# The late slot tiles of a routed layer: more DMA transposes, probabilities folded into the rows, ReLU and sum as one operation of VectorE

## The chip, the cores and the metric

The kernel runs on one core of one Trainium2 chip. A core has five engines: TensorE (PE for its products, PEld for its weight loads), VectorE (DVE), ScalarE (ACT), GpSimd (POOL) and SyncE (SP). All DMAs, from whichever engine's queue, are carried by 16 DMA engines. Time is the device time of one execution in microseconds (us), and lower is better.

## The reference

Two layers run over x of 2 x 2048 rows of 512. Each is a cross attention to a context of 128 rows and a feed forward part, with residual sums. Only the last part matters here, the feed forward part of the second layer, in which each row is sent to one of eight experts:

```python
xn = (x - mean) / sqrt(var + 1e-5)
probs = softmax(xn @ Wg + bg)
idx = argmax(probs)
p = probs[idx]
e = idx % 8
h = relu(xn @ We[e] + be[e])
x = x + h * p
```

The probability p is positive, so p * relu(z) equals relu(p * z). Everything is fp32 in this part.

## The kernel before, in words

There are 32 tiles of 128 rows (NT), called x tiles, and they stay in SBUF (xw, 516 columns each: 512 of data, then the mean, the reciprocal deviation, the probability p and a zero). The first layer and the second layer's attention run over these tiles until about 1440 us. A finished tile is written to a buffer in DRAM (x_dram), with its four extra columns.

The rows are then put in order by expert. A *slot tile* is 128 rows that all belong to one expert; there are 39 of them, numbered j = 0 to 38 here and called slots. The first NJA = 15 are formed when 22 of the 32 x tiles are done (routing(True)) and hold full slots only; the other 24 (NJB) are formed at the end (routing(False)), and there an expert's last slot can be partly empty, and the last slots wholly. For each slot the routing gives the expert's number, the rows to fetch (row), and the place in the output of each (tok). The change sets in at LATE = NJA + 3 = slot 18.

The work on a slot is spread over several turns of expert(j), which are unrolled. The order on TensorE, VectorE, ScalarE and GpSimd is the program's own order (a manual schedule); only semaphores hold an instruction back. SP's queue has the DMA transposes.

- gathered(j + 4), L1157 to L1162: GpSimd issues an indirect DMA that fetches slot j + 4's rows, with their mean, deviation and probability, into one of six buffers (xw[0] to xw[5]).
- turned_x2(j + 1), L1178 to L1185: slot j + 1's centred rows come into transposed form (128 features on the partitions, in four blocks). There are two ways. In the first, TensorE transposes four 128x128 blocks (L116) and ScalarE evicts them from PSUM (L1185), adding RAISE = 4.0 to the first feature of each block by a bias column. In the second, by_dma(j), the rows have gone through a DMA transpose (which works on 16-bit data: split, L825 to L829, lets VectorE part the fp32 words into halves and SP issue the transpose), and ScalarE joins the halves (joined, L831). Before the change every odd slot from 5 on goes this way.
- the product, L1193 to L1195: four blocks of 128 features times the expert's weights, each fp32 product in two passes, so eight matmuls a slot into one PSUM bank of 512 columns (pz). The expert's bias is not added in a separate step: RAISE makes the first feature of each block larger by 4, and the weights have had rows added that carry the bias to match.
- centered_x(j + 3), L1164 to L1172: VectorE centres and scales slot j + 3's rows (L104 in center). For a slot that goes by DMA it then adds RAISE to four columns (L1171), and calls split.
- the end of slot j, L1197 to L1203: ScalarE computes relu(p * z) from PSUM (L1198), VectorE adds x (L1199), GpSimd issues an indirect DMA that scatters the rows to the output (L1200). Empty places have a row number beyond the output and are left out by the DMA.

On VectorE, then, slot j's sum stands behind slot j + 3's centring, RAISE and split. On GpSimd's queue gathers and scatters take turns: gather j + 4, scatter j, gather j + 5, scatter j + 1. The scatters all write the tensor out, and the gathers all read x_dram. The PSUM banks for transposes and products come from one pool of four buffers (psm, tag m).

Of the kernel before, what the change touches and what calls it, by code (L numbers as in the profile page):

```python
# [16 lines left out]
U16 = mybir.dt.uint16  # L17
I8 = mybir.dt.int8
AF = mybir.ActivationFunctionType
ALU = mybir.AluOpType  # L20
# [4 lines left out]
P = 128  # L25
B, S, T, D = 2, 2048, 128, 512
ND = D // P
# [16 lines left out]
NJA = NTA - (NE - 1)  # L44
# [4 lines left out]
RAISE = 4.0  # L49
# [14 lines left out]
def two_layers(ctx: ExitStack, tc: tile.TileContext, a, out):  # L64
    nc = tc.nc
# [16 lines left out]
    raised = const.tile([P, 1], F32, name="raised")  # L82
# [3 lines left out]
    xw = [xres.tile([P, DX], F32, name=f"x{n}") for n in range(NT)]  # L86
# [16 lines left out]
    def center(dst, x, mean, scale):  # L103
        nc.vector.tensor_scalar(dst, x, mean, scale, ALU.subtract, ALU.mult)  # L104
# [7 lines left out]
    def transposed(psum, src, n=ND):  # L112

        pt = psum.tile([P, n, P], F32, name="pt", tag="m")
        for c in range(n):
            nc.tensor.transpose(pt[:, c, :], src[:, c * P : (c + 1) * P], ident)  # L116
        return pt
# [707 lines left out]
    def split(x, planes):  # L825
        nc.vector.tensor_copy(
            planes.rearrange("p (h f) -> p h f", h=2), x.bitcast(U16).rearrange("p (f h) -> p h f", h=2)
        )
        nc.sync.dma_start(out=x.bitcast(U16).rearrange("p (b q) -> p b q", q=P), in_=planes, transpose=True)  # L829

    def joined(dst, x):  # L831
        nc.scalar.copy(  # L832
            dst.bitcast(U16).rearrange("p c (q h) -> p h c q", h=2),
            x.bitcast(U16).rearrange("p (h c q) -> p h c q", h=2, c=ND),
        )
# [181 lines left out]
    def part(n, shape, dtype=F32, at=0):  # L1017

        size = math.prod(shape)
        v = xw[n][:, at : at + (size * mybir.dt.size(dtype) + 3) // 4]  # L1020
        if dtype is not F32:
            v = v.bitcast(dtype)[:, :size]
        if len(shape) == 1:
            return v
        names = "abc"[: len(shape)]
        return v.rearrange(f"p ({' '.join(names)}) -> p {' '.join(names)}", **dict(zip(names, shape)))
# [128 lines left out]
    ring = {}  # L1155

    def gathered(j):  # L1157
        if j < NJ:
            nc.gpsimd.indirect_dma_start(
                out=xw[j % 6], out_offset=None, in_=x_dram[: (NTA if j < NJA else NT) * P, :],  # L1160
                in_offset=bass.IndirectOffsetOnAxis(ap=tile_of[j][2], axis=0),
            )  # L1162

    def centered_x(j):  # L1164
        if j < NJ:
            x = xw[j % 6]
            xn = part(6 + j % 3, [D])
            center(xn, x[:, :D], x[:, D : D + 1], x[:, D + 1 : D + 2])
            if by_dma(j):
                first = xn.rearrange("p (c q) -> p c q", c=ND)[:, :, 0:1]  # L1170
                nc.vector.tensor_scalar(first, first, RAISE, None, ALU.add)  # L1171
                split(xn, part(24 + j // 2 % 2, [2 * D], U16))  # L1172

    def by_dma(j):

        return j > 4 and j % 2 == 1

    def turned_x2(j):  # L1178
        if j < NJ and by_dma(j):
            ring[j] = part(9 + j % 3, [ND, P])  # L1180
            joined(ring[j], part(6 + j % 3, [D]))
        elif j < NJ:
            pt = transposed(psm, part(6 + j % 3, [D]))
            ring[j] = part(9 + j % 3, [ND, P])
            nc.scalar.activation(ring[j], pt, AF.Identity, bias=raised)  # L1185

    def expert(j):

        te, tok, _ = tile_of[j]
        gathered(j + 4)  # L1190
        turned_x2(j + 1)
        e = nc.tensor.value_load(te, min_val=0, max_val=NE - 1)
        pz = psm.tile([P, D], F32, name="pz", tag="m")  # L1193
        for c in range(ND):
            nc.tensor.matmul(pz, ring[j][:, c, :], we[:, bass.ds(e, 1), c, :], start=(c == 0), stop=(c == ND - 1))  # L1195
        centered_x(j + 3)
        x, acc = xw[j % 6], part(12 + j % 3, [D])  # L1197
        nc.scalar.activation(acc, pz, AF.Relu, scale=x[:, D + 2 : D + 3])  # L1198
        nc.vector.tensor_tensor(acc, acc, x[:, :D], ALU.add)  # L1199
        nc.gpsimd.indirect_dma_start(  # L1200
            out=out_rows, out_offset=bass.IndirectOffsetOnAxis(ap=tok, axis=0),
            in_=acc, in_offset=None, bounds_check=NT * P - 1, oob_is_err=False,
        )  # L1203
# [32 lines left out]
    for n in range(NT):  # L1236
# [55 lines left out]
        if not ahead:  # L1292

            expert(n - NT + NB1)
# [18 lines left out]
        if n == NT - NB1 - 1:  # L1313
            for j in range(3):
                centered_x(j)
            turned_x2(0)
# [4 lines left out]
    picked(NT - 2)  # L1321
    gated(NT - 2)()
    expert(2)
    turned2(NT - 1)
    expert(3)
    logits(NT - 1)
    picked(NT - 1)
# [48 lines left out]
```

## Time and profile before

| what | value |
|---|---|
| time, median of 3 runs | 1597.74 us (1596.93 to 1598.61) |
| time of the profiled execution | 1599.43 us |
| its span, first to last instruction | 1597.4 us |
| granted TensorE clock, mean | 0.995 |
| PE, DVE, ACT, POOL busy over the span | 97%, 75%, 45%, 37% |
| first and last product of a slot (L1195) | 1408.7 and 1586.8 us |
| last scatter issued | 1589.12 us |
| slot 18's first product | 1507.7 us |

The span runs from the first to the last instruction; the time of an execution also has what lies around it (2.0 us here). A line of the timeline gives the start, the duration, the engine, the line of the program, the operation, the names out<-in, their shapes where there are any, and a count; in brackets stands how long the engine was idle before it and what ended that. Names such as x stand for any of the xw tiles: gathered rows, centred rows, transposed rows and sums all lie in them, so the line number tells them apart. A line such as L104 or L826 stands in a helper that several parts call.

### The profile page before, as it was taken

The page shows a single profiled execution, that of the slowest core. Times are in us where ns is not written, and L with a number is a line of the kernel's source. Part 1 is how long each engine was busy: PE and PEld are TensorE (multiplying, and loading weights), DVE is VectorE, ACT ScalarE, POOL GpSimd, SP SyncE. Part 2 cuts the span into 40 slices and gives each one's busy share as a digit, 9 for nine tenths or more (in the row PEclk, how much of TensorE's full clock was granted, in tenths as well). Part 3 has the DMA queues.
Part 4 walks back from the last instruction along what each step waited for, and adds up shares of the span by engine and source line. Part 5 has one row for each costly group of instructions (what it writes and reads, how often), then busy time and mean ns, then how long its engine had stood idle before and what let it go on. Part 6 is the DMA issues. An engine that isn't in the chain of part 4 may idle for free. (4 is left out here: it accounts for less than half of the span.)

```text
span 1597.4 us, 26167 instructions
## 1 busy us (share of the span) xinstructions
PE 1551.3 (97%) x9542; PEld 909.1 (57%) x9542; DVE 1192.5 (75%) x2333; ACT 720.4 (45%) x1537; POOL 586.8 (37%) x580
## 2 busy tenths in 40 slices
PE   7999999999999999999999999999999999999997
PEld 5655555555555555544444466666666666654443
DVE  3467777777777886589986678888888888877442
ACT  1222222222222222243335566777777776763442
POOL 2232222222222222110005654555565444544553
PEclk9999999999999999999999999999999999999999
DMA  9511212111111220367768734221311111114553
GB/s 321 188 37 41 47 40 47 40 47 40 51 46 41 59 60 1 117 169 205 179 173 278 271 132 143 48 47 34 55 45 36 41 28 41 41 47 131 162 162 89
DMA packets 180571, 150.90 MB, mean 94 GB/s; under 512 B 97089, under 2 KB 144665, under 8 KB 180444
## 3 DMA queue, kind: packets, MB, share of 16 engines
q1 hardware_dynamic: 170188, 127.25, 28.5%
q0 software_dynamic: 6240, 18.70, 3.8%
q10 hardware_dynamic: 4016, 3.29, 0.9%
q8 instruction: 76, 1.25, 0.3%
q14 instruction: 51, 0.42, 0.1%
HBM read 89.97 MB, written 41.79 MB: 82 GB/s over the span
## 5 line engine op out<-in xcount | busy, mean ns | idle before, releaser
L419 ACT ACTIVATE pr<-sc 128x1024 f32<-128x1024 f32 x64 | 65.6, 1024 | 421.6 <-PE sc L414 421.4
L393 PE MATMUL pq<-xnT,wq 128*128 128x256 f32 x1024 | 254.4, 391 | 0.0
L451 PE MATMUL pw<-wo,att 128*128 128x512 f32 x512 | 230.8, 593 | 0.0
L393 PEld LDWEIGHTS pq<-xnT,wq 128*128 128x128 f32 x1024 | 184.4, 189 | 67.1 <-issue 44.0
L914 ACT ACTIVATE s<-s,mx 128x128 f32<-128x128 f32 x512 | 175.3, 388 | 28.1 <-DVE mx L905 28.1
L923 POOL TENSOR_TENSOR s<-s,rs 128x1024 f32<-128x1024 f32 x64 | 120.9, 1903 | 149.6 <-DVE rs L922 149.1
L403 POOL TENSOR_TENSOR q<-rt,rt 128x256 f32<-128x256 f32 x64 | 46.7, 730 | 339.7 <-DVE rt L402 335.2
L451 PEld LDWEIGHTS pw<-wo,att 128*128 128x128 f32 x512 | 96.9, 190 | 96.4 <-issue 89.9
L441 DVE RECIPROCAL rd<-sc 128x256 f32<-128x256 f32 x64 | 112.4, 1757 | 46.5 <-PE sc L435 46.5
L1195 PE MATMUL pz<-we,x 128*128 x312 | 139.3, 598 | 1.8 <-ACT x L832 1.6
L872 PE MATMUL pq<-xT,wq 128*128 128x256 f32 x512 | 122.6, 382 | 0.0
L978 PE MATMUL pl<-wgate,xnT 128*128 128x512 f32 x256 | 116.7, 599 | 0.0
L955 PE MATMUL pw<-wo,oT 128*128 128x512 f32 x256 | 115.2, 592 | 0.7 <-ACT oT L946 0.7
L872 PEld LDWEIGHTS pq<-xT,wq 128*128 128x128 f32 x512 | 96.0, 190 | 33.1 <-issue 20.3
L398 DVE TENSOR_TENSOR rt<-pq,rope_cos 128x256 f32<-128x256 f32 x64 | 27.0, 422 | 104.2 <-PE pq L393 104.2
L749 ACT ACTIVATE gate<-pg,gsc 128x512 f32<-128x512 f32 x88 | 60.5, 687 | 93.9 <-PE pg L744 84.0
L1195 PEld LDWEIGHTS pz<-we,x 128*128 128x128 f32 x312 | 58.2, 192 | 68.4 <-issue 65.2
L92 DVE BATCH_NORM_STATS2 st<-x 128x6 f32<-128x512 f32 x130 | 89.4, 688 | 6.0 <-DMA x<-in_ctx 3.8
L744 PE MATMUL pu<-xqT,wuT 128*128 128x512 bf16 x352 | 90.3, 379 | 2.6 <-DVE h L752 2.4
L744 PE MATMUL pg<-xqT,wgT 128*128 128x512 bf16 x352 | 90.3, 379 | 0.0
L900 DVE SCALAR_TENSOR_TENSOR s<-sc,keep 128x1024 f32<-128x1024 f32 x64 | 78.1, 1220 | 14.3 <-PE sc L892 9.1
L955 PEld LDWEIGHTS pw<-wo,oT 128*128 128x128 f32 x256 | 48.6, 190 | 55.3 <-issue 53.6
(226 smaller groups left out, 2811.8 us busy)
## 6 DMA issues: line engine op xcount, KB each, us to landing
h_dram<-h SPq DMA_DIRECT2D x88, 256.0 KB
hq<-h_dram SPq DMA_DIRECT2D x31, 704.0 KB
x_dram<-x SPq DMA_DIRECT2D x32, 258.0 KB
x<-in_x SPq DMA_DIRECT2D x32, 256.0 KB
we<-in_L_ffn_We SPq DMA_DIRECT2D x8, 1024.0 KB
xnT<-in_x_turned SPq DMA_DIRECT2D x14, 512.0 KB
along<-stat_dram SPq DMA_DIRECT2D x14, 256.0 KB
w_in<-in_L_ffn_w_gate SPq DMA_DIRECT2D x11, 256.0 KB
```

Source lines behind the costliest of these rows:

```text
L92: nc.vector.bn_stats(out=st, in_=x)
L393: nc.tensor.matmul(pq, wqs[c // 2][:, c % 2, par, g * P : (g + 1) * P], xnTs[k][:, c, :], start=(c == 0), stop=(c == ND - 1))
L441: nc.vector.reciprocal(rd, sc[:, 0, B0:])
L451: nc.tensor.matmul(pw, atts[u][:, f, t * P : (t + 1) * P], wo[:, 2 * g + f, :], start=(g == 0 and f == 0), stop=(g == NG - 1 and f == 1),)
L744: nc.tensor.matmul(dst, w[:, c, i * P : (i + 1) * P], xqTs[blk][:, c, :], start=(c == 0), stop=(c == ND - 1),)
L872: nc.tensor.matmul(pq, wq1[:, c, f * P : (f + 1) * P], xTs[blk][:, c, :], start=(c == 0), stop=(c == ND - 1))
L900: nc.vector.scalar_tensor_tensor(s, sc[:, 2 * half : 2 * half + 2].rearrange("p r c k -> p (r c) k"), -MASKED, keeps[n].unsqueeze(1).to_br ...
L914: nc.scalar.activation(s[:, h, :], s[:, h, :], AF.Exp, bias=mx[:, h : h + 1], **accum)
L923: nc.gpsimd.tensor_tensor(s, s, rs.unsqueeze(2).to_broadcast([P, 8, T]), ALU.mult)
L955: nc.tensor.matmul(pw, os_[n][:, c, :], wo1[:, c, :], start=(c == 0), stop=(c == ND - 1))
L978: nc.tensor.matmul(pl, xn2T[n][:, c, :], wgate[:, c, :], start=(c == 0), stop=(c == ND - 1))
L1195: nc.tensor.matmul(pz, ring[j][:, c, :], we[:, bass.ds(e, 1), c, :], start=(c == 0), stop=(c == ND - 1))
```

## The change

It touches slots 18 to 38 alone.

- Which slots go by DMA: there j % 3 > 0 (19, 20, 22, 23, ... 37, 38), where it was the odd ones. The halves' buffers become three (24 + j % 3) in place of two.
- The probability is multiplied into the rows: VectorE forms scale times probability in the spare column (rp), and centring uses it, so that the product is already p * z. What RAISE adds must then be p * RAISE, and it is added to the rows by VectorE in every slot (scalar_tensor_tensor on four columns), not only in those that go by DMA; ScalarE's eviction of a TensorE transpose (L1185) becomes a plain copy.
- ReLU and sum: in place of ScalarE's activation (L1198) and VectorE's sum (L1199) there is one scalar_tensor_tensor of VectorE, max(pz, 0) + x, which reads PSUM.

```diff
+    LATE = NJA + 3
+
     def centered_x(j):
+
         if j < NJ:
-            x = xw[j % 6]
-            xn = part(6 + j % 3, [D])
-            center(xn, x[:, :D], x[:, D : D + 1], x[:, D + 1 : D + 2])
+            x, xn = xw[j % 6], part(6 + j % 3, [D])
+            r, p = x[:, D + 1 : D + 2], x[:, D + 2 : D + 3]
+            first = xn.rearrange("p (c q) -> p c q", c=ND)[:, :, 0]
+            if j >= LATE:
+                rp = x[:, D + 3 : D + 4]
+                nc.vector.tensor_tensor(rp, r, p, ALU.mult)
+                center(xn, x[:, :D], x[:, D : D + 1], rp)
+                nc.vector.scalar_tensor_tensor(first, p.to_broadcast([P, ND]), RAISE, first, ALU.mult, ALU.add)
+            else:
+                center(xn, x[:, :D], x[:, D : D + 1], r)
+                if by_dma(j):
+                    nc.vector.tensor_scalar(first, first, RAISE, None, ALU.add)
             if by_dma(j):
-                first = xn.rearrange("p (c q) -> p c q", c=ND)[:, :, 0:1]
-                nc.vector.tensor_scalar(first, first, RAISE, None, ALU.add)
-                split(xn, part(24 + j // 2 % 2, [2 * D], U16))
+                split(xn, part(24 + j // 2 % 2 if j < LATE else 24 + j % 3, [2 * D], U16))
 
     def by_dma(j):
 
-        return j > 4 and j % 2 == 1
+        return j % 3 > 0 if j >= LATE else j > 4 and j % 2 == 1
 
     def turned_x2(j):
...
             ring[j] = part(9 + j % 3, [ND, P])
-            nc.scalar.activation(ring[j], pt, AF.Identity, bias=raised)
+            if j >= LATE:
+                nc.scalar.copy(ring[j], pt)
+            else:
+                nc.scalar.activation(ring[j], pt, AF.Identity, bias=raised)
 
     def expert(j):
...
         x, acc = xw[j % 6], part(12 + j % 3, [D])
-        nc.scalar.activation(acc, pz, AF.Relu, scale=x[:, D + 2 : D + 3])
-        nc.vector.tensor_tensor(acc, acc, x[:, :D], ALU.add)
+        if j >= LATE:
+            nc.vector.scalar_tensor_tensor(acc, pz, 0.0, x[:, :D], ALU.max, ALU.add)
+        else:
+            nc.scalar.activation(acc, pz, AF.Relu, scale=x[:, D + 2 : D + 3])
+            nc.vector.tensor_tensor(acc, acc, x[:, :D], ALU.add)
```

## The prediction

> **Views, and what bounds the kernel.** I read the page first, its engine shares.
>
> ```profile
> PE 1551.3 (97%) x9542; PEld 909.1 (57%) x9542; DVE 1192.5 (75%) x2333; ACT 720.4 (45%) x1537; POOL 586.8 (37%) x580
> ```
>
> TensorE looks like the bound of the whole, but the change acts only from slot 18 on, so I read that stretch alone. Slots are found by counting: there are 39 scatters of L1200, the one at 1589.12 is slot 38. Slot 18's gathered rows are centred at 1500.47. Next comes the table by stretches, cut at the PE transposes, so that each row holds two slots (stretch, its length, busy time of PE, PEld, DVE, ACT, POOL, clock, DMA share, GB/s).
>
> ```profile
> 1504.30:1511.60 7.30, 7.30 (x22) 3.42 (x21) 3.05 (x6) 3.28 (x5) 3.78 (x4) 1.00 0.61 177
> ...
> 1563.60:1571.90 8.30, 7.50 (x22) 3.39 (x20) 3.16 (x6) 3.11 (x5) 4.48 (x5) 1.00 0.60 161
> 1571.90:1580.20 8.30, 7.57 (x20) 3.46 (x20) 3.16 (x6) 3.12 (x5) 3.44 (x4) 1.00 0.51 124
> ```
>
> At the start of the stretch TensorE has no gap and two slots take 7.30; at its end two slots take 8.30 with the same work. Something else has become late by then. The waits from 1475 to the end (total us, times, longest) say what:
>
> ```profile
> DVE x L104 <- DMA x<-x_dram,x: 52.6, 26, 2.9
> POOL out_x L1200 <- DMA out_x<-x,x: 18.4, 11, 2.2
> ACT x L832 <- DMA x<-x: 15.7, 10, 2.6
> DVE x L1199 <- ACT x L1198: 9.9, 7, 3.2
> PEld pz L1195 <- ACT x L832: 2.6, 4, 1.1
> ```
>
> VectorE waits for gathers, and scatters wait for the scatter before them: each scatter writes the same output tensor, so each is held until its predecessor has landed. Gather and scatter take turns on POOL's queue, so a late scatter delays the next gather. POOL's timeline shows the pace:
>
> ```profile
> 1510.87 1.05 POOL L1200 DMA_INDIRECT out_x<-x,x  x1 [2.12 <-DMA out_x<-x,x]
> 1512.23 1.35 POOL L1159 DMA_INDIRECT x<-x_dram,x  x1 [0.30 <-ACT x L1198]
> 1514.49 1.02 POOL L1200 DMA_INDIRECT out_x<-x,x  x1 [0.91 <-DMA out_x<-x,x]
> ...
> 1518.43 1.02 POOL L1200 DMA_INDIRECT out_x<-x,x  x1 [1.52 <-DMA out_x<-x,x]
> ...
> 1522.20 1.02 POOL L1200 DMA_INDIRECT out_x<-x,x  x1 [1.46 <-DVE x L1199]
> ```
>
> These are the scatters of slots 17, 18, 19 and 20, at intervals of 3.62, 3.94 and 3.77. Over all scatters from slot 16 (1506.44) to 35 (1580.09) the interval after an even slot is 4.15 (ten, sum 41.49), after an odd slot 3.57 (nine, sum 32.16). TensorE needs 7.30 / 2 = 3.65 a slot. So **the ring of scatters is the bound from about slot 16**, TensorE trails it, and by the last four slots stands still for it. Even slots are slower because just before scatter j VectorE splits slot j+3, which is odd and goes through the DMA transpose, whose transfer then flies beside the scatter. One round, with slot 27 brought in and slot 24 written:
>
> ```profile
> 1529.54 1.02 POOL L1200 DMA_INDIRECT out_x<-x,x  x1 [1.08 <-DVE x L1199]
> 1530.87 0.98 POOL L1159 DMA_INDIRECT x<-x_dram,x  x1 [0.30 <-ACT x L1198]
> ...
> 1534.64 0.60 DVE L104 TENSOR_SCALAR x<-x 128x512 f32<-128x512 f32 x1 [2.47 <-DMA x<-x_dram,x]
> ...
> 1535.27 0.17 DVE L1171 TENSOR_SCALAR x<-x 128x4 f32<-128x4 f32 x1
> 1535.47 0.79 DVE L826 COPY x<-x 128x1024 uint16<-128x1024 uint16 x1
> 1536.18 0.67 DVE L1199 TENSOR_TENSOR x<-x,x 128x512 f32<-128x512 f32 x1
> ...
> 1537.13 1.02 POOL L1200 DMA_INDIRECT out_x<-x,x  x1 [1.38 <-DVE x L1199]
> ...
> 1539.89 1.35 ACT L832 COPY x<-x 128x1024 uint16<-128x1024 uint16 x1 [1.65 <-DMA x<-x]
> ```
>
> The second loop is seen here: scatter 22 to gather 27 1.33, to its centring 3.77, centring to split 0.83, to the sum 0.71, the sum 0.67, to scatter 24 0.28: 7.59 for two slots, nearly the 4.15 + 3.57 = 7.72 of the ring. Both loops bind in turn.
>
> **The change, part by part** (slots 18 to 38).
>
> Fewer transposes on TensorE. Of these 21 slots 11 were turned by TensorE, now 7 (18, 21, ... 36). Four transposes lie between 1503.87 and the next product at 1504.31, 0.44; four slots save 1.76. I count it as nothing: what hides it is TensorE's own lateness behind the ring. Had TensorE the lead, it would be worth 1.76.
>
> More slots by DMA: 14 in place of 10, so four more splits (0.69 each, VectorE), four more transposes in SP's queue (from issue at 1536.40 to the joining at 1539.89, 3.49), four more joinings (1.34, ACT) in place of four evictions (0.68, ACT). Nothing else stands in SP's queue after 1455; ACT waits 45.1 us for products in this stretch, so its work is covered. What is on the path is the slower kind of scatter interval. Those with a DMA slot three ahead were 10 of the 19 intervals of slots 16 to 34; now they are slots 16, 17, 19, 20, 22, 23, 25, 26, 28, 29, 31, 32 and 34, 13 of 19. 3 x (4.15 - 3.57) = **+1.74**. This assumes that two DMA slots in a row disturb no more than single ones; from below, if the difference came from the order of slots alone, 0.
>
> The split is where a page speaks against the change. The row: the gather at 1512.23 took 1.35 beside a split (0.69 from 1512.05), others 0.98. The Trainium skill (SBUF — State Buffer, Who interferes with whom) says that a VectorE copy in its two-port mode holds the port pair that GpSimd shares, and GpSimd is blocked for the whole instruction. By the rule four more splits could hold four queue entries for up to 0.69, 2.8 in all; by the row 4 x 0.37 = 1.5. Neither is added here.
>
> The product of scale and probability, on one column. An operation on 128x1 takes 0.15 (L986), and the one that reads its result as a scalar starts 0.19 after it (L1002 at 1441.60, L1003 at 1441.79). It stands between the gather's landing and the centring, so it lengthens the second loop by 0.19 in each slot. The raise of the first columns as a scalar_tensor_tensor is priced by L1145's 0.18, against 0.17 at L1171 for DMA slots; for TensorE's slots it is new, 0.20 with its start, where the loop has over 0.8 to spare (no split).
>
> ReLU and sum as one operation of VectorE. No row has just this; L956 (PSUM and SBUF, 128x512) takes 0.69, L821 (scalar_tensor_tensor, 128x512) 0.75. I take 0.70, nearest to L956, against 0.69 for L1199. ScalarE's L1198 goes (21 x 0.68). In the body it isn't worth anything: slot 24's ReLU started at 1533.63, right behind its product, and its sum at 1536.18, held by centring and split. The waits on L1198 (9.9) that it would remove fell before slot 18. The sum now waits for TensorE itself; behind it stand the next slot's product, centring and split, and it is ready long before. The PSUM buffer is freed by the sum, some 2.75 later (slot 32: ReLU ends 1564.09, sum 1566.84); with four buffers, and four taken in three slots, product 33 (1563.63) would need slot 30's sum, done at 1558.89. 4.7 to spare, so nothing.
>
> So the second loop grows by 0.19 + 0.01 a DMA slot. From below 0, where the ring binds; from above 0.20 for each two slots over 18 slots, 1.8. The ring of two slow intervals is 8.3, the loop 7.6 to 7.8, so most is hidden: **+0.5**.
>
> The end. Slot 38 is now a DMA slot. Its centring started at 1577.79, when the gather had landed; + 0.19 + 0.58 + 0.20 + 0.69 + 0.14 gives an issue at 1579.6; 3.5 (as slot 27) to 4.3 (slot 37, issued 1574.53, joined from 1578.87) and the joining 1.34 give a product at 1584.4 to 1585.3, before 1583.79: +0.6 to +1.5. Then ReLU and sum, 1587.43 to 1588.84, 1.41, become 0.73: -0.68. **Between -0.1 and +0.8, I take +0.3**.
>
> Sum: 1.74 + 0.5 + 0.3 = **+2.5**. The profiled execution took 1599.43, its span 1597.4 and 2.0 around it; the span would be 1599.9. The median of the runs, 1597.74, is 1.7 below the profiled time; 1597.74 + 2.5 = **1600.2**.
>
> **Rivals.** *TensorE is the bound after all.* For it: no gap at TensorE until 1563. Against: scatters at 3.86 a slot against its 3.65. Then 1.76 and the 0.68 at the end come through: 1595.3; if the 2 x 1.0 of the last two pairs went too, 1593.3. It decides if scatter intervals fall below 3.6.
>
> *The DMA transposes get in each other's way* (slower). Two DMA slots follow each other at 3.9, and a transpose takes 3.5 to 4.3 from issue to joining. From scatter j-5 to scatter j by way of the transpose: 1.33 + 3.77 + 0.19 + 0.63 + 0.20 + 0.93 + 3.49 + 1.35 + 0.05 + product and its end 3.7 + 0.70 + 0.28 = 16.6 for five slots, 3.3 each: spare 2.9. It decides from 6.4 a transpose on. At 7.0 (two in line) 20.1 / 5 = 4.02 in place of 3.86, 20 slots x 0.16 = 3.2 more: 1603.4. For it: the 4.3 of slot 37. Against: the DMA share is 0.6, not 1.
>
> *The disturbance is no matter of transposes*, and the added VectorE work is covered: 1597.74 to 1598.2. For it: the two kinds of interval are read from one order of slots, in which even and odd never change places. Against: ten of ten even intervals are longer than the odd ones beside them.
>
> **How the numbers follow.** Forecast 0.50 (its own range 1598.7 to 1602.3), TensorE 0.18, transposes in line 0.22, no effect 0.10. What a measurement of this kernel can tell from no change is about 0.2%, 3.2 us: 1594.5 to 1600.9. Of the forecast about 0.32 lie within that and 0.18 above; of the TensorE case 0.12 below and 0.06 within. Faster 0.12, same 0.32 + 0.06 + 0.10 = 0.48, slower 0.18 + 0.22 = 0.40. The range takes the transposes' case to 1604 and half the TensorE case, to 1594.5.
>
> **What would show it.** Right: scatters about 3.95 apart, longer after slots with a DMA slot three ahead; three slots on TensorE 11.5 to 12 where its work is 10.7; more waiting of TensorE for L832's successor; product to first sum unwaited. Wrong: intervals below 3.7 and a TensorE without gaps (faster), transposes of 6 and more from issue to joining (slower), or a sum much above 0.75.

## The result, and the profile after

The changed kernel takes 1601.49 us in the median of 21 runs, the kernel before 1598.26 in 21 runs beside them: a ratio of 1.0018, 95% interval 1.0012 to 1.0025, so it is slower by 2.9 us (1.9 to 4.0). The forecast was +2.5. One execution in a later run, of the changed kernel with views, took 3219.12 and is left out of its ratio. The profiled execution's span is 1599.6, before 1597.4. From slot 18's first product (1507.08, before 1507.74) to the end of the span it takes 92.5, before 89.7: +2.9, so the time is lost in the slots that the change touches.

The engine shares of the page hardly move:

```profile
PE 1549.6 (97%) x9526; PEld 904.7 (57%) x9526; DVE 1199.8 (75%) x2369; ACT 709.3 (44%) x1516; POOL 585.6 (37%) x580
```

TensorE has 1.7 us less work (four transposed slots, forecast 1.76), ScalarE 11.1 less, VectorE 7.3 more, and yet the time rises. The table by stretches, now of three slots each because that is the new rhythm (stretch, its length, busy time of PE, PEld, DVE, ACT, POOL, clock, DMA share, GB/s):

```profile
1507.10:1517.80 10.70, 10.70 (x29) 4.92 (x28) 5.92 (x14) 3.95 (x4) 5.96 (x6) 1.00 0.55 150
1517.80:1530.80 13.00, 11.24 (x29) 4.90 (x28) 5.87 (x14) 3.11 (x3) 5.84 (x7) 1.00 0.63 166
1530.80:1542.90 12.10, 11.34 (x30) 4.91 (x29) 5.84 (x14) 3.11 (x3) 5.56 (x6) 1.00 0.61 153
...
1566.30:1578.10 11.80, 11.23 (x30) 4.92 (x29) 5.96 (x14) 3.27 (x3) 6.05 (x6) 1.00 0.67 174
```

The first three slots take 10.70 without a gap, which is the pace that the saved transposes allow; every later three take 11.6 to 13.0. Before, TensorE had hardly a gap until 1563; now gaps stand in every stretch from 1517.80 on. The busy times of 11.0 to 11.3 beside a need of 10.7 also hold short waits between products. The waits from 1475 to the end:

```profile
ACT x L832 <- DMA x<-x: 41.7, 11, 6.0
DVE x L1175 <- DMA x<-x_dram,x: 39.8, 21, 4.0
POOL out_x L1217 <- DVE x L1213: 22.4, 12, 2.9
...
PEld pz L1209 <- ACT x L832: 12.0, 11, 1.8
POOL out_x L1217 <- DMA out_x<-x,x: 10.7, 7, 2.2
```

The scatters' waits have to be read beside a line of the kernel before that the prediction doesn't show. It stands in the same view as the others, above the ring's 18.4:

```profile
POOL out_x L1200 <- DVE x L1199: 22.1, 16, 2.3
```

Two shifts matter. The wait of TensorE's weight loads for joined rows rose from 2.6 to 12.0. And the scatters' waits moved further to the sum: for the scatter before, eleven waits (18.4) have become seven (10.7), while from slot 18 on twelve scatters (22.4) wait for VectorE's new sum (L1213). In the same views from 1505 on the kernel before has ten waits for the scatter before (16.7) and eleven for the sum (13.9), the changed one seven (10.7) and fourteen (25.5, L1213 and the two of L1216). The second loop of the prediction, gather to sum, bound about as often as the ring before; now it binds twice as often. One round, with slot 26 brought in and slot 23 written:

```profile
1526.83 1.02 POOL L1217 DMA_INDIRECT out_x<-x,x  x1 [2.66 <-DVE x L1175]
1528.15 1.06 POOL L1159 DMA_INDIRECT x<-x_dram,x  x1 [0.30 <-issue]
...
1528.43 18.61 SPq L829 DMA_TRANSPOSE x<-x  x4
...
1530.37 1.02 POOL L1217 DMA_INDIRECT out_x<-x,x  x1 [1.16 <-DMA out_x<-x,x]
...
1533.00 0.16 DVE L1175 TENSOR_TENSOR x<-x 128x1 f32<-128x1 f32 x1 [4.05 <-DMA x<-x_dram,x]
1533.26 0.55 DVE L104 TENSOR_SCALAR x<-x 128x512 f32<-128x512 f32 x1
1533.46 1.33 ACT L832 COPY x<-x 128x1024 uint16<-128x1024 uint16 x1 [5.75 <-DMA x<-x]
...
1534.65 0.68 DVE L1213 SCALAR_TENSOR_TENSOR x<-pz,x 128x512 f32<-128x512 f32 x1
...
1535.61 1.02 POOL L1217 DMA_INDIRECT out_x<-x,x  x1 [2.94 <-DVE x L1213]
```

The row of SPq stands for four issues merged into one; the first is at 1528.43. The round took 8.78 for two slots, where the round shown of before took 7.59. The gather of 1528.15 needed 4.85 to VectorE's first instruction (before 3.77), and the transpose issued at 1528.43 was joined only at 1533.46, after 5.03 (before 3.49). Both were in flight at once, and the scatter of 1530.37 came between. From scatter 16 to scatter 35 the profiled execution takes 76.67, before 73.65: +3.0. From there to the last scatter nothing more is lost (8.97, before 9.02).

### The profile page after: what moved, and what is told of

The parts are those of the page before. It is cut to its first block, busy times and chain, and to the rows that moved or that the text cites. A ratio compares the mean times of both kernels' runs of the same rounds, so it can differ in the third digit from the quotient of the medians.

```text
span 1599.6 us, 26125 instructions
## 1 busy us (share of the span) xinstructions
PE 1549.6 (97%) x9526; PEld 904.7 (57%) x9526; DVE 1199.8 (75%) x2369; ACT 709.3 (44%) x1516; POOL 585.6 (37%) x580
## 5 line engine op out<-in xcount | busy, mean ns | idle before, releaser
L810 PE MATMUL py<-wdT,hb 128*128 128x512 bf16 x352 | 78.7, 383 | 2.3 <-DVE hb L804 1.5
```

The costliest lines, as they stand in the source:

```text
L810: nc.tensor.matmul(py, hbs[n][:, i, :], wdT[:, i, :], start=(i == 0), stop=(i == NI - 1))
```

## The experiments

All ratios are against the kernel before, run on the same chip beside them. 0.001 is 1.6 us. Intervals in parentheses are 95%. Diffs show the lines that matter; LATE and the third buffer for the halves, an import, and new buffers in DRAM are left out of some.

**One half of the change at a time.** The transposes alone:

```diff
-        return j > 4 and j % 2 == 1
+        return j % 3 > 0 if j >= LATE else j > 4 and j % 2 == 1
```

> The kernel before with only the rule changed that says which slots from 18 on go by DMA (two of three, three buffers for the halves); probability, ReLU and sum as before. Theory R (the ring of scatters decides, and an interval is longer when the slot three ahead goes by DMA): 3 more long intervals x 0.58 = +1.7, and slot 38 by DMA at the end +0.6 to +1.5, so +2.3 to +3.2 us against before. Theory T (TensorE decides): four fewer transposes, -1.8. Theory Q (the added VectorE work is what made the changed kernel slower): 0.

1.0021 (1.0013 to 1.0030), +3.4 us (2.1 to 4.8). That is just above theory R's range, which the interval covers; T and Q are out as the whole.

The fold alone (probability in the rows, ReLU and sum on VectorE), in the changed kernel:

```diff
-        return j % 3 > 0 if j >= LATE else j > 4 and j % 2 == 1
+        return j > 4 and j % 2 == 1
```

> The changed kernel with every odd slot by DMA, as before; the probability in the rows and ReLU and sum on VectorE stay. Theory R: 0 to +0.5 in the body, -0.7 at the end for the merged ReLU and sum, so -0.7 to -0.2 us against before. Theory T: -0.7. Theory Q: all of the +2.9 that the changed kernel shows, less nothing: +2 to +3.

0.9994 (0.9985 to 1.0003), -1.0 us (-2.4 to +0.5). Q is refuted: the added VectorE work costs nothing that shows. The halves sum to +2.4, the whole is +2.9. So the additional transposes are what makes the changed kernel slower.

**Fewer transposes by DMA.** One of three slots:

```diff
-        return j % 3 > 0 if j >= LATE else j > 4 and j % 2 == 1
+        return j % 3 == 1 if j >= LATE else j > 4 and j % 2 == 1
```

> The changed kernel with one of three slots by DMA from 18 on (19, 22, ... 37) and 14 turned by TensorE. Theory R: 7 long intervals of 19 in place of 10, -1.7 against before, end -0.7, second loop up to +0.5, TensorE's need 3.43 + 2/3 x 0.44 = 3.72 just under the mean interval of 3.76: -1.5 to -2.5 us against before. Theory T: three more transposes on TensorE +1.3 and the end -0.7: +0.6. Theory Q: +2 to +3 as in the changed kernel.

0.9996 (0.9986 to 1.0006), -0.6 us. This misses R's range on the upper side: the interval (-2.2 to +1.0) holds the upper part of it, and the +0.6 of T as well. Q is refuted again.

**The ring taken away.** First with a second tensor in the kernel before, then without leaving anything out, by views of the output that are declared disjoint:

```diff
-            out=out_rows, out_offset=bass.IndirectOffsetOnAxis(ap=tok, axis=0),
+            out=aside if j >= NJA + 3 and j % 2 else out_rows, out_offset=bass.IndirectOffsetOnAxis(ap=tok, axis=0),
```

> The kernel before, whose odd slots from 18 on are scattered to a buffer of their own in DRAM and not to the output, so that their rows are missing from the result and a scatter no longer waits for the one just before it. Theory R: the ring goes; what is left is TensorE's 3.65 a slot or the second loop (7.2 to 7.6 for two slots) in place of 3.86: -1.2 to -3.8 us against before, and no wait of a scatter on a scatter from slot 19 on. Theory T: the ring was no bound, 0.

0.9989 (0.9980 to 0.9998), -1.8 us (-3.2 to -0.3). From slot 19 on no scatter waits for another in its profile.

```diff
-    out_rows = out.rearrange("b t d -> (b t) d")
+    out_views = dram_disjoint_views(out.rearrange("b t d -> (b t) d"), 4)
-            out=out_rows, out_offset=bass.IndirectOffsetOnAxis(ap=tok, axis=0),
+            out=out_views[j % 4], out_offset=bass.IndirectOffsetOnAxis(ap=tok, axis=0),
```

> The kernel before, with the scatters going through four views of the output that are declared disjoint (each row of the output belongs to one slot), so that a scatter waits only for the fourth before it. All slots write the output, nothing is left out. Theory R1 (the ring of scatters is the bound before): as in the run with two tensors, -1.2 to -2.5 us against before, TensorE at 3.65 to 3.75 a slot. Theory R2 (the second loop, gather, centring, split, sum, scatter, binds as much): -0.5 or less.

0.9975 (0.9964 to 0.9986), -4.0 us (-5.8 to -2.2). Both say that the waits of scatter for scatter cost time in the kernel before, and T, for which the ring was no bound, is refuted. How much of it is the late slots' isn't shown. The second tensor touches only slots 18 on and gave -1.8; the views reach all 39 slots and gave more than R1's range. Nor do the profiled executions place the 4.0: from slot 18's first product to the end of the span the one with views takes 89.1, the one before 89.7. In the table by stretches of two slots (columns as above) TensorE runs at its own 7.30 in most of them until 1566, but not in all:

```profile
1507.20:1514.50 7.30, 7.30 (x21) 3.44 (x20) 3.25 (x6) 3.16 (x4) 4.14 (x4) 1.00 0.63 177
...
1521.80:1529.70 7.90, 7.61 (x21) 3.46 (x20) 3.60 (x7) 3.15 (x4) 4.46 (x5) 1.00 0.59 157
...
1544.30:1551.60 7.30, 7.30 (x21) 3.43 (x20) 3.25 (x6) 3.26 (x4) 4.20 (x4) 1.00 0.59 157
...
1559.00:1566.30 7.30, 7.30 (x21) 3.42 (x20) 2.32 (x5) 3.21 (x4) 4.14 (x4) 1.00 0.63 174
1566.30:1574.80 8.50, 7.51 (x21) 3.46 (x20) 3.81 (x8) 3.13 (x4) 3.99 (x4) 1.00 0.59 157
```

The same views in the changed kernel:

> The changed kernel with the same four views. Theory R1 (what the change lengthened is the ring): the ring goes with its price, -1 to -3 us against before and below the kernel before with views by the TensorE transposes saved, up to 1.8. Theory R2 (what the change lengthened is the second loop, by the product on one column and by more splits): it stays at 7.6 to 7.8 for two slots where a slot goes by DMA, 3.7 to 3.9 a slot, 0 to -1.5 us against before, and above the kernel before with views.

1.0001 (0.9990 to 1.0012), +0.2 us. R1 failed here: without the ring the change costs 1.0001 - 0.9975 = 0.0026, 4.2 us (1.7 to 6.6), which isn't seen to be less than the 2.9 with it. What the change costs isn't carried by the ring alone. R2's range, 0 to -1.5, lies within the interval (-1.6 to +1.9), so R2 isn't ruled out here.

**The second loop taken away.** In the changed kernel VectorE sums before it centres:

```diff
-        centered_x(j + 3)
+        if j < LATE:
+            centered_x(j + 3)
         x, acc = xw[j % 6], part(12 + j % 3, [D])
...
             nc.vector.tensor_tensor(acc, acc, x[:, :D], ALU.add)
+        if j >= LATE:
+            centered_x(j + 3)
```

> The changed kernel with one order changed: from slot 18 on VectorE does slot j's ReLU and sum before the centring and split of slot j + 3, not behind them, so that a scatter no longer waits for a gather. The ring of scatters stays. Theory R1: nothing gained, +2 to +3 us against before as in the changed kernel. Theory R2: the second loop goes, scatters come 3.6 to 3.8 apart by the ring alone, -2 to 0 us against before.

1.0009 (0.9999 to 1.0019), +1.4 us (-0.2 to +3.0), between the two theories: inconclusive. Then both loops away, this order and the views:

> The changed kernel with both: sum before centring from slot 18 on, and four views of the output. Both loops are gone, and TensorE is left with 3.43 a slot and 0.44 for each of six transposed slots, 71.2 us from slot 18's product to slot 38's where before took 76.0: -3 to -5 us against before by R1 and R2 alike. If it is no faster than the changed kernel, neither loop was the bound and something else, such as the DMA transposes, sets the pace.

1.0041 (1.0028 to 1.0054), +6.6 us, the slowest of all, where both theories had -3 to -5. With neither loop there, the transposes and, less so, the gathers had become slow. The trace's packets show how. I parted the DMA transposes from slot 18 on by whether gather or scatter packets (over 2 KB) ran between a transpose's first and last packet; "alone" is fewer than eight such packets. Times in us are from issue (SP's queue) to the start of the joining, which mostly follows the landing as ScalarE is idle; the last two columns are from a gather's start to its last packet and to the centring, means of slots 19 to 35.

| kernel | alone: number, mean | beside gather or scatter: number, mean (range) | gather to its last packet | gather to centring |
|---|---|---|---|---|
| before | 0 | 10, 3.90 (3.46 to 4.42) | 3.21 | 3.65 |
| changed | 3, 3.17 | 11, 3.90 (3.33 to 5.03) | 3.25 | 3.93 |
| before, views | 9, 3.22 | 1, 3.55 | 3.22 | 3.63 |
| changed, views | 7, 3.24 | 7, 5.12 (3.43 to 7.00) | 3.70 | 4.50 |
| changed, views, sum first | 3, 3.19 | 11, 5.65 (4.67 to 7.20) | 4.18 | 6.65 |

The last column isn't the gather's time alone. With the fold the centring starts 0.24 behind the product on one column; and with the sum first VectorE waits for TensorE before it centres, as the waits of the last kernel from 1505 on show:

```profile
DVE x L1215 <- PE pz L1210: 46.5, 20, 5.8
...
DVE x L1176 <- DMA x<-x_dram,x: 2.5, 1, 2.5
```

L1215 is the sum there, L1176 the product on one column: a gather holds VectorE up once, TensorE twenty times. A transpose alone has its data packets through in 1.42. In the last row those beside gathers and scatters take 3.51 on average, and the gathers' last packets come 1.0 later than before. That made theory C, collision at the DMA engines.

**Count against coincidence.** The next two kernels have the same transposes (every odd slot), the same fold and the same views, and differ in one order on VectorE, the one of the diff above.

> The kernel before with four views of the output and with the changed kernel's probability in the rows and ReLU and sum on VectorE, every odd slot by DMA. Theory C (what costs is a DMA transpose that shares the DMA engines with a gather or scatter; in the kernel before with views nine of ten run alone and take 3.2 from issue to joining): they stay alone, and the fold gives its 0 to -1: -4 to -5.5 us against before. Theory V (the added VectorE work costs once the scatters are free): slower than the kernel before with views by 1 or more.

0.9975 (0.9965 to 0.9986), -4.0 us. Its middle falls on C's edge. It is the ratio of the views alone, so the fold adds nothing that can be told; V's 1 us or more isn't seen, but lies within the noise.

> As the run before this one (views, fold, every odd slot by DMA), but the sum before the centring on VectorE. The number of DMA transposes is the same; they now are issued about when a gather follows the scatter. Theory C: they collide as in the changed kernel with sum first and views, 4.5 and more from issue to joining, gathers over 4.5, +2 to +5 us against the run without the changed order. Theory N (only the number of transposes costs): within 1 us of it.

0.9999 (0.9990 to 1.0007): 0.0024, 3.8 us (1.6 to 6.1) above the run before it. N, within 1 us, is refuted; C's +2 to +5 holds. In the profiled executions slot 18's first product to the end of the span takes 87.2 in the first and 90.8 in the second, so the difference lies in the late slots. From the first one's timeline, one round, with the gather first:

```profile
1534.74 0.97 POOL L1160 DMA_INDIRECT x<-x_dram,x  x1 [0.30 <-issue]
...
1537.76 8.48 SPq L830 DMA_TRANSPOSE x<-x  x2
1538.13 0.15 DVE L1176 TENSOR_TENSOR x<-x 128x1 f32<-128x1 f32 x1
...
1538.49 1.02 POOL L1218 DMA_INDIRECT out_x<-x,x  x1 [2.78 <-DVE x L1176]
...
1540.97 1.34 ACT L833 COPY x<-x 128x1024 uint16<-128x1024 uint16 x1 [4.61 <-DMA x<-x]
```

And from the second one's:

```profile
1534.99 1.42 POOL L1221 DMA_INDIRECT out_x<-x,x  x1 [1.13 <-DVE x L1176]
...
1536.43 9.85 SPq L830 DMA_TRANSPOSE x<-x  x2
1536.71 0.97 POOL L1160 DMA_INDIRECT x<-x_dram,x  x1 [0.30 <-issue]
...
1540.86 1.34 ACT L833 COPY x<-x 128x1024 uint16<-128x1024 uint16 x1 [5.07 <-DMA x<-x]
```

The rows of SPq merge issues again; the one meant is the first, at the row's start. In the first kernel the gather of 1534.74 has arrived (its slot is handled from 1538.13) before the transpose's packets move, and the next scatter is issued at 1538.49; the transpose is joined 3.21 after its issue. In the second the scatter of 1534.99 and the gather of 1536.71 stand on both sides of the transpose's issue, and it is joined after 4.43. Over all slots 9 of 10 ran alone in the first (mean 3.18), none in the second (mean 4.52), and the gathers' last packets come 3.12 and 3.48 after their start. It is mostly not the transpose's data that are late in the second: they take 1.65 on average. But the last of the 32 packets of 4 bytes that close each transpose comes 2.65 after its first packet, when alone 1.43.

The rival here is the order itself: it puts the split behind the sum, and so behind TensorE. An estimate from the second trace speaks against it. With 3.2 from issue to joining and the joining's 1.34, all ten DMA slots would be joined before TensorE is through with what stands ahead of them; with their own times TensorE stands still in six places, 3.3 us in all, against one place and 1.0 in the first trace. The Trainium skill (DMA: Bandwidth & Descriptors, Issuing engines are not separate DMA queues) says that DMAs from the SP, ACT and POOL queues run on the same 16 engines and interleave; this pair of runs agrees: where the transposes meet gathers and scatters, they come 1.3 us later on average.

**The fastest.** One of three by DMA with views and fold:

> Views, fold, and one of three slots by DMA from 18 on. TensorE's need is 3.72 a slot against 3.65 with every second slot: 20 x 0.07 = +1.4 against the run with every odd slot by theory C, if there the transposes run alone; if they don't, fewer collisions make it the faster one.

0.9971 (0.9962 to 0.9980), -4.6 us, the fastest measured, with every row of the output written; it can't be told from 0.9975. In its profile none of the seven transposes ran alone, but they took only 3.26 to 3.82: to meet a gather or a scatter is not always dear.

**Without the scatters' bytes.**

```diff
-            out=out_rows, out_offset=bass.IndirectOffsetOnAxis(ap=tok, axis=0),
-            in_=acc, in_offset=None, bounds_check=NT * P - 1, oob_is_err=False,
+            out=asides[j % 4] if j >= LATE else out_views[j % 4], out_offset=bass.IndirectOffsetOnAxis(ap=tok, axis=0),
+            in_=acc[:, :8] if j >= LATE else acc, in_offset=None, bounds_check=NT * P - 1, oob_is_err=False,
```

> The changed kernel with four views, but from slot 18 on only 8 of the 512 columns are scattered, to a buffer aside; the late slots' rows are missing from the output. The transposes, the order and VectorE's work are those of the changed kernel with views. Theory C: with the scatters' bytes gone a transpose shares the engines with gathers alone, 3.2 to 4 from issue to joining in place of up to 7.0, TensorE near 3.6 a slot, -3 to -6 us against the changed kernel with views (so -3 to -6 against before). Theory V or theory Q (VectorE's added work): no change, 0 against before.

1.0010 (0.9998 to 1.0021), +1.6 us (-0.3 to +3.4): a miss for C, and no gain over the changed kernel with views (1.0001). No change is what V and Q had said. Q is refuted by the fold alone, and V isn't seen in the pair above with every odd slot by DMA; with two of three slots by DMA V stays untested. The profiled execution took 1596.48 where the median is 1602.38, so its trace, with transposes of 3.14 to 4.41, doesn't show what the usual ones do. Whether a scatter disturbs by its bytes or by its number of packets, or whether the gathers do it alone, stays open.

## Why the prediction was right, point by point

- **What bounds the kernel before** (the ring, with TensorE trailing): right in part. Taking the ring away in the late slots gave -1.8 us, in all slots -4.0; that rules out the rival in which TensorE decides, and the four transposes saved on it brought nothing, as counted. But "the bound from about slot 16" says too much: from 1505 on eleven scatters waited for the sum and ten for the scatter before, so the two loops that the prediction says bind in turn are the better reading.
- **More slots by DMA**, +1.74 in the body and +0.6 to +1.5 at the end: alone it measured +3.4 (2.1 to 4.8), just above the sum. In the profile after, the intervals with a DMA slot three ahead are 4.14 on average (13), as sized; the other six are 3.81, not 3.57. With the transposes alone it is 3.92 and 4.07: scatter 16 to 35 grew by 1.8 there, as forecast, but not by the rule that the forecast counted with. The end there is 9.18 from scatter 35 to the last, before 9.02: +0.2, less than taken. The step's condition, that two DMA slots in a row disturb no more than single ones, did not hold in every round: single rounds of 8.78 occur where transpose, gather and scatter meet. And its mechanism was too narrow. I read the longer interval as a property of the ring; the views in the changed kernel show that a cost stays (4.2 us) when the ring goes. In the changed kernel itself it is seen at TensorE, which from slot 18 to 38 stands still (gaps over 0.05) for 5.2 us, before for 1.6, each time ahead of a slot that comes by DMA. An estimate with 3.2 from issue to joining for all transposes leaves 1.7 of the 5.2 and nothing of the 1.6: about two thirds is transposes that took longer than alone, the rest transposes issued late.
- **The loop through gather and sum**, +0.5 with 0.19 a slot: the centring starts 0.19 to 0.27 behind the product on one column, 0.24 on average (1533.00 to 1533.26 in the round above), and this loop rather than the ring ends most waits of scatters. In the profiled executions the body lost 3.0 where 1.74 + 0.5 = 2.24 was forecast. What this loop costs by itself no run shows: the fold alone, which has it, came out at -1.0.
- **ReLU and sum on VectorE**: 0.68 measured at L1213 against 0.70 taken; it waits for TensorE twice (6.5 us in all) in 21 slots, so "unwaited" holds but for these. The fold alone measured -1.0 (-2.4 to +0.5), forecast 0.5 - 0.68.
- **The end**, +0.3: last scatter minus scatter 35 is 8.97, before 9.02, so nothing. Slot 38's transpose, with nothing beside it, took 3.18, under both values taken (3.5 and 4.3), which makes up for the rest.
- **The blocked port**: the Trainium skill's rule (SBUF — State Buffer, Who interferes with whom) would have held gathers up at four more splits if they met. The gathers' time on POOL's queue did not rise: median 0.98 after 1505, before 1.05. Leaving it out of the sum was right here.
- **Transposes in each other's way**, the slower rival: not as told, one behind another. The transpose that follows a DMA slot's transpose is often the quick one (slots 20, 26 and 38: 3.17, 3.16, 3.18). What delays them in the pair of runs is gathers and scatters. The signs named for it, 6 and more from issue to joining, appear only once views free the scatters.
- **What would show it**: scatters 3.95 apart were 4.04 on average; three slots of TensorE 11.5 to 12 were 11.6 to 13.0 from the second three on.

So the amount came out right partly by luck. The interval of 4.15, read where the slot three ahead goes by DMA, had the price of a transpose beside a gather or scatter in it, whatever it was put down to. And the parts that missed offset each other: the transposes cost a little more than their sum, the fold and the end a little less.

## What to carry to other kernels

A transpose moved from TensorE to DMA is paid for in rows that come late, and here the price depended on what else was in flight: compare its time from issue to use when alone (3.2 here) with when it meets a gather or scatter (up to 7.2), and look for an order in which they don't meet before adding more of them. If writes to one tensor wait for each other although they touch different rows, declare them disjoint first; here that alone was worth 4.0 us (2.2 to 5.8), more than the change as a whole cost. Taking one wait away can move transfers into each other's way: the kernel with both loops cut was the slowest of all. And before a transfer is called slow, see whether its user was waiting for it or for something else.

## What the runs showed of the hardware that was not expected

A DMA transpose of 128 rows of 1024 16-bit elements has its data packets through in 1.42 us when alone and in 3.51 on average (1.71 to 4.89) among gather and scatter packets, in the kernel with sum first and views; the gathers there had their last packet 4.18 after their start, before 3.21. Even where the data take no longer than alone, the closing packets of 4 bytes can: in the kernel with views, fold and sum first slot 27's data took 1.38, but it was joined after 4.43. ScalarE's plain copy of 128x512 from PSUM took 0.59 (L1197, median), the same eviction with a bias column 0.68 (L1185).
